# One of four subtractions as an adding DMA, in a graph-attention layer on one core

## The chip, the cores and the metric

The kernel runs on one core of a Trainium2 chip. A core has five engines that work side by side, each with its own queue of instructions in order: PE (TensorE, matrix products), DVE (VectorE), ACT (ScalarE), POOL (GpSimd) and SP (SyncE, which here issues DMAs). DMAs run on 16 DMA engines; SP's and POOL's DMAs are issued from those engines' queues. Engines wait for each other and for DMAs by semaphores. Data lies in SBUF (128 partitions), products in PSUM. The metric is the device time of one execution in microseconds (us); less is better.

## The reference

Four layers of a graph network over 32 graphs of 512 nodes with 64 features, all with the same adjacency matrix. The change touches only the last layer, a graph attention with eight heads and one output head:

```python
def gat_layer(x, graph, W, b):
    h = x @ W
    s = jnp.einsum('bnd,bmd->bnm', h, h) * graph
    s = jnp.where(s == 0.0, NEG_INF, s)
    a = jax.nn.softmax(s, axis=2)
    return jnp.einsum('bnm,bmd->bnd', a, h) + b
...
heads = jax.vmap(lambda W, b: gat_layer(flow_x, graph, W, b))(Wh, bh)
...
x = jax.nn.leaky_relu(cat, negative_slope=0.01)
out = gat_layer(x, graph, W_out, b_out)
return jax.nn.leaky_relu(out, negative_slope=0.01)
```

Each softmax needs, for each node, the greatest of its scores, which is subtracted before the exponential. Scores are symmetric, so the kernel takes maxima along one axis and subtracts them along the other.

## The kernel before

Layers 0 to 2 take the first 460 us or so. The rest is layer 3, as a pipeline of 144 units: 128 units of the class `Heads` (32 graphs, four units each, a unit being two heads of one graph) and 16 of `Out` (the output head of two graphs). A unit has scores of two 512x512 matrices, held as four row blocks r = 0 to 3; each block is a tile `p_att` of 128 partitions by 1024 floats (`self.p[r]`, from the pool `pbuf` of 14 buffers).

The steps of a unit:

- `scores(r)`: PE multiplies into the PSUM tile `s_ps` (two buffers).
- `maxima(r)` (L379): one DVE instruction for each half of the block writes the negated, masked scores to `p_att` and the least of each row, which is minus the greatest score, to a column of `top`.
- `spread_out` (L386, L389): DVE transposes `top` into `top_t`; SP writes it with four small DMAs to `top_row` in DRAM.
- `spread_in` (L395): SP loads that row, repeated on all 128 partitions, into `topb` (512 KB in SBUF, two buffers).
- `shift(r)` (L401): POOL subtracts `topb` from block r.
- `exps(r)` (L404): ACT takes exp(-p) of block r.
- `totals` (L420 to L432): PE sums the columns, DVE transposes the sums, ACT copies them to `parts`.
- `values(j)` (L410), `recips`, `normalize` (L438 to L450): PE multiplies with the values, DVE divides.
- `y_pe`, `y_act` (L538), `y_dve` (L546): PE multiplies with the head's weights, ACT and DVE make the leaky ReLU, `cat`.
- For the output: `product` (PE, L570), `keep_product`, `make_v`, `make_gs` (POOL, L589), `back`, `back_pool` (POOL), `store` (SP).
- `make_hx`, `make_g` (ACT copies, L522), `features` (small ACT steps) prepare later units.

The order is written out by hand. `flow_period(t)` emits the instructions of period t, and the order in which it emits them is the order on every engine's queue (the schedule is manual for all five engines). In period t, `now` is unit t, `unit(1)` the unit before, `unit(2)` the one before that, and `ahead` the next. So the maxima of blocks 2 and 3 of unit t and its `spread_out` and `spread_in` are emitted after `exps(0)`, `y_act` and `exps(1)` of `unit(1)`; then follow `y_dve`, the first maxima of the next unit, `shift(2)`, `exps(2)`, POOL's and SP's output steps, `totals`, `shift(3)`, `exps(3)`, and the rest. Waits between engines are put in by the framework from what is written and read.

`nc.gpsimd.dma_start` issues a DMA from POOL's queue; the kernel uses it before only for some weights at its start (L94 to L127).

Of the kernel before, what the change touches and what calls it, by code (L numbers as in the profile page):

```python
# [10 lines left out]
OP = mybir.AluOpType  # L11
# [3 lines left out]
P = 128  # L15
# [7 lines left out]
def fast_form(  # L23
# [25 lines left out]
    nc = tc.nc  # L49
    B, N, F = x.shape  # L50
    C = N // P
# [264 lines left out]
    class Pair:  # L316
# [67 lines left out]
        def spread_out(self):  # L384
            t = tiny.tile([P, 32], F32, name="top_t")
            nc.vector.transpose(t, self.top)  # L386
            self.top_row = dram.tile([2 * C, P], F32, name="top_row")
            for q in range(Q):
                nc.sync.dma_start(  # L389
                    self.top_row[:, q * 32 : (q + 1) * 32], t[q * 32 : q * 32 + 2 * C, :]  # L390
                )
# [6 lines left out]
            )  # L398

        def shift(self, r):  # L400
            nc.gpsimd.tensor_tensor(self.p[r], self.p[r], self.topb, OP.subtract)  # L401

        def exps(self, r):
            nc.scalar.activation(self.p[r], self.p[r], AF.Exp, scale=-1.0)  # L404
# [227 lines left out]
    def any_zero():  # L632

        def across(src, rows, name):
            ps = ps_m.tile([P, P], F32, name=name, tag="m")
            n = src.shape[0]
            nc.tensor.transpose(ps[:rows, :n], src, ident[:n, :n])
            return ps[:rows, :n]

        own = tiny.tile([P, 1], F32, name="own")  # L640
        nc.vector.tensor_reduce(own, least, AX.X, OP.min)
        two = tiny.tile([1, 2], F32, name="two")
        nc.vector.tensor_reduce(two[:, 0:1], across(own, 1, "own_ps"), AX.X, OP.min)
        best = tiny.tile([B // 2, 2], F32, name="best")
        nc.vector.tensor_reduce(
            best,
            across(least_out, B // 2, "out_ps").rearrange("b (k f) -> b k f", k=2),
            AX.X, OP.max,
        )
        worst = tiny.tile([B // 2, 1], F32, name="worst")  # L650
        nc.vector.tensor_reduce(worst, best, AX.X, OP.min)
        nc.vector.tensor_reduce(
            two[:, 1:2], across(worst, 1, "worst_ps"), AX.X, OP.min
        )
        flag = tiny.tile([1, 1], F32, name="flag")
        nc.vector.tensor_reduce(flag, two, AX.X, OP.min)
        nc.vector.scalar_tensor_tensor(
            again, flag, 0.0, unsound, op0=OP.is_equal, op1=OP.max
        )
# [6 lines left out]
    def planned(units, products):  # L666

        class Nothing:
            def __getattr__(self, name):
                return lambda *args: None  # L670

        nothing = Nothing()

        def period(t):
            def unit(lag):
                return units[t - lag] if 0 <= t - lag < len(units) else nothing

            now, ahead = unit(0), unit(-1)
            for r in range(2, C):
                now.scores(r)  # L680
            unit(3).y_pe()
            unit(1).shift(0)
            unit(1).exps(0)
            unit(3).y_act()
            if t - 1 in products:
                products[t - 1].keep_product()
            unit(1).shift(1)
            unit(1).exps(1)
            for r in range(2, C):
                now.maxima(r)  # L690
            now.spread_out()
            now.spread_in()
            for r in range(2):
                ahead.scores(r)
            unit(3).y_dve()
            for r in range(2):
                ahead.maxima(r)
            unit(-3).features(3)
            unit(3).back()
            unit(1).shift(2)  # L700
            unit(1).exps(2)
            unit(4).back_pool()
            unit(-2).make_gs()
            unit(4).store()
            unit(2).totals()
            unit(1).shift(3)
            unit(1).exps(3)
            for j in range(C):
                unit(2).values(j)
            u = products.get(t)  # L710
            if u:
                u.product()
            unit(2).recips()
            unit(3).back_dve()
            unit(2).normalize()
            unit(1).make_v()
            unit(-3).make_hx()
            unit(-2).make_g()
            for step in range(3):
                unit(step - 6).features(step)  # L720
            if t == len(units):
                any_zero()

        return period
# [1061 lines left out]
```

## Time and profile before

| What | Value |
|---|---|
| Median of 3 runs | 2175.14 us (2174.02 to 2175.47) |
| The profiled execution's own time | 2177.9 us |
| Its span, first to last instruction | 2176.1 us |
| Mean granted TensorE clock | 0.992 |
| `topb` loads | 144 of 512 KB |
| DMA queues' busy share (hardware queue q1) | 12.5% of 16 engines |
| POOL's subtraction, L401 | 576 times 2376 ns |
| ACT's exponential, L404 | 576 times 1057 ns |
| DVE's maxima, L379 | 1152 times 685 ns |

A row of the profile's groups gives line, engine, operation, the tile written and the tiles read, shapes and count, then busy time in us and the mean of one in ns, then the engine's idle time just before these instructions and what ended most of it. A row of a timeline gives the start in us from the span's start, how long the engine took for the merged group, engine, line, operation, tiles and count. "POOLq" and "SPq" are those engines' instruction sequencers, which issue DMAs. The chain of work that ended last is followed back from the last instruction, at each step to what released it.

### The profile page before, as it was taken

What the parts mean: (1) busy time and instruction counts of PE and PEld (TensorE: products, weight loads), DVE (VectorE), ACT (ScalarE), POOL (GpSimd) and SP (SyncE); (2) the same over time, 40 slices, a digit from 0 to 9 for tenths busy, and PEclk for the clock granted to TensorE, in tenths of its full rate; (3) what the DMA queues carried; (4) which work ended last, traced back from release to release, by engine and by line L of the source; (5) the groups of instructions that cost most, each with busy time, mean ns of one, the idle gap of its engine ahead of it and who ended that gap; (6) DMA issues with size and microseconds to landing.
All of it is one profiled execution on the core that took longest, in us unless ns stands there. A gap on an engine that the chain in (4) does not pass through costs nothing.

```text
span 2176.1 us, 34386 instructions
## 1 busy us (share of the span) xinstructions
PE 2108.7 (97%) x12190; PEld 840.5 (39%) x12190; DVE 1661.6 (76%) x4241; ACT 1294.9 (60%) x2520; POOL 1420.0 (65%) x665
## 2 busy tenths in 40 slices
PE   7999999989999999999999999999999999999996
PEld 4666776733333333333333333333333333333332
DVE  6799997668787877777777787877787787878774
ACT  3444433347676767675767676766676676766554
POOL 2000000048787878787878787878787877878786
PEclk9999999899999999999999999999999999999999
DMA  5000000001111111111111111111111111111112
GB/s 134 1 1 2 1 1 1 1 30 50 40 49 54 49 45 54 40 54 40 54 49 55 40 54 40 54 40 54 50 54 40 40 50 50 48 41 50 40 49 51
DMA packets 54565, 89.87 MB, mean 41 GB/s; under 512 B 30008, under 2 KB 35296, under 8 KB 54256
## 3 DMA queue, kind: packets, MB, share of 16 engines
q1 hardware_dynamic: 53872, 87.39, 12.5%
q8 instruction: 97, 1.59, 0.3%
q0 software_dynamic: 512, 0.20, 0.1%
q14 instruction: 84, 0.69, 0.1%
HBM read 81.73 MB, written 4.78 MB: 40 GB/s over the span
## 4 chain that ended last, share of the span: by engine, by line
PE 55%; DVE 27%; ACT 9%; POOL 3%; issue 3%; DMA 2%; DVEq 0%; SPq 0%; POOLq 0%; ACTq 0%
DVE p_att L379 15%; PE av L410 13%; PE nt_ps L833 7%; PE s_ps L367 7%; PE tot_ps L420 7%; PE acc L925 6%; PE gT_ps L570 5%; DVE cat L546 3%; POOL p_att L401 3%; PE g_ps L510 3%; ACT parts L432 2%; DVE recb L443 2%; DVE o_att L450 2%; ACT p_att L404 2%; DVE tot_t L427 2%
## 5 line engine op out<-in xcount | busy, mean ns | idle before, releaser
L401 POOL TENSOR_TENSOR p_att<-p_att,topb 128x1024 f32<-128x1024 f32 x576 | 1348.8, 2376 | 394.2 <-DMA topb<-top_row 254.4
L379 DVE CUSTOM_DVE_ANT_0 p_att<-s_ps,flow_neg 128x512 f32<-128x512 f32 x1152 | 724.5, 685 | 160.0 <-PE s_ps L367 159.9
L404 ACT ACTIVATE p_att<-p_att 128x1024 f32<-128x1024 f32 x576 | 607.1, 1057 | 216.5 <-POOL p_att L401 207.8
L367 PE MATMUL s_ps<-hx,g 64*128 64x512 f32 x2048 | 527.2, 612 | 17.5 <-ACT hn L474 5.8
L410 PE MATMUL av<-p_att,hn 128*64 128x512 f32 x2048 | 468.2, 599 | 0.0
L367 PEld LDWEIGHTS s_ps<-hx,g 64*128 64x128 f32 x2048 | 174.1, 185 | 322.3 <-DVE top L379 184.3
L420 PE MATMUL tot_ps<-p_att,ones 128*32 128x512 f32 x2304 | 281.2, 602 | 2.8 <-ACT p_att L404 2.5
L410 PEld LDWEIGHTS av<-p_att,hn 128*64 128x64 f32 x2048 | 135.8, 137 | 327.8 <-issue 327.8
L1001 POOL TENSOR_TENSOR x<-x,bias_b 128x512 f32<-128x512 f32 x16 | 20.3, 1275 | 280.1 <-DVE hn L775 280.1
L546 DVE SCALAR_TENSOR_TENSOR cat<-y_ps,bh,cat 128x512 f32<-128x512 f32 x256 | 177.8, 736 | 18.5 <-ACT cat L538 15.0
L538 ACT ACTIVATE cat<-y_ps,bh 128x512 f32<-128x512 f32 x256 | 160.8, 679 | 18.7 <-PE y_ps L528 17.9
L438 DVE TENSOR_REDUCE rec_flow<-parts 128x16 f32<-128x32 f32 x144 | 27.1, 188 | 176.1 <-ACT parts L432 176.1
L522 ACT COPY g<-g_ps 128x512 f32<-128x512 f32 x128 | 68.6, 588 | 154.0 <-PE g_ps L510 153.7
L430 ACT COPY parts<-tot_t 128x16 f32<-128x16 f32 x144 | 31.3, 217 | 181.4 <-DVE tot_t L427 181.4
L528 PE MATMUL y_ps<-o_att,wh_sb 64*128 64x512 f32 x512 | 133.5, 597 | 4.0 <-DVE o_att L450 3.1
L420 PEld LDWEIGHTS tot_ps<-p_att,ones 128*32 128x32 f32 x2304 | 60.5, 109 | 191.7 <-issue 108.2
L432 ACT COPY parts<-tot_t 32x16 f32<-32x16 f32 x576 | 123.8, 215 | 6.7
L925 PE MATMUL acc<-v,s 64*128 64x65 f32 x2048 | 124.2, 280 | 0.7 <-DVE s L911 0.4
L427 DVE STREAM_TRANSPOSE tot_t<-tot_ps 128x512 f32<-128x512 f32 x144 | 102.2, 710 | 29.1 <-PE tot_ps L420 29.1
L925 PEld LDWEIGHTS acc<-v,s 64*128 64x128 f32 x2048 | 121.3, 195 | 5.9 <-DVE o L941 1.2
L833 PE MATMUL nt_ps<-adj_t,hn 128*128 128x512 f32 x256 | 116.1, 596 | 0.8 <-DVE hn L797 0.8
L570 PE MATMUL gT_ps<-cat,wo_sb 128*64 128x512 f32 x512 | 112.6, 592 | 0.0
(176 smaller groups left out, 2021.8 us busy)
## 6 DMA issues: line engine op xcount, KB each, us to landing
topb<-top_row SPq DMA_DIRECT2D x144, 512.0 KB
top_row<-top_t SPq DMA_DIRECT2D x576, 1.0 KB
out_dram<-y SPq DMA_DIRECT2D x32, 128.0 KB
x<-in_x_dram SPq DMA_DIRECT2D x3, 1024.0 KB
x<-in_x_dram SPq DMA_DIRECT2D x4, 256.0 KB
adj_raw<-in_adj_dram SPq DMA_DIRECT2D x1, 1024.0 KB
mask<-mask SPq DMA_DIRECT2D x4, 256.0 KB
wh_sb<-in_L_gnn_Wh_dram SPq DMA_DIRECT2D x2, 256.0 KB
```

The costliest lines, as they stand in the source:

```text
L367: nc.tensor.matmul(ps[:, k], lhsT=g[halves(k), r * P : (r + 1) * P], rhs=x[halves(k), :], start=True, stop=True,)
L379: nc.vector.tensor_tensor_reduce(out=self.p[r][:, k], in0=ps[:, k], in1=flow_neg[:, r], scale=-1.0, scalar=BIG, op0=OP.add, op1=OP.min, ac ...
L401: nc.gpsimd.tensor_tensor(self.p[r], self.p[r], self.topb, OP.subtract)
L404: nc.scalar.activation(self.p[r], self.p[r], AF.Exp, scale=-1.0)
L410: nc.tensor.matmul(self.av[halves(k), :], lhsT=self.v(k, j), rhs=self.p[j][:, k], start=(j == 0), stop=(j == C - 1),)
L420: nc.tensor.matmul(ps[q : q + 32, :], lhsT=ones, rhs=self.p[j][:, k], start=(j < 2), stop=(j >= 2),)
L432: nc.scalar.copy(self.parts[q * 32 : (q + 1) * 32, 1], one[(q ^ 1) * 32 : ((q ^ 1) + 1) * 32])
L538: nc.scalar.activation(self.cat[:, k], self.y[k], AF.Identity, bias=bh01[:, h : h + 1], scale=0.01)
L546: nc.vector.scalar_tensor_tensor(self.cat[:, k], self.y[k], bh[:, h : h + 1], self.cat[:, k], op0=OP.add, op1=OP.max,)
L570: nc.tensor.matmul(ps[halves(k), :], lhsT=wo_sb[:, h, :], rhs=Heads.cat[self.b + k, h], start=(h == 0), stop=(h == H - 1),)
L833: nc.tensor.matmul(p, lhsT=lhs(k), rhs=adj_t[:, k, :], start=(k == 0), stop=(k == C - 1))
L925: nc.tensor.matmul(self.acc[k][:, r], lhsT=self.s[b // 2][halves(k), b % 2, r * P : (r + 1) * P], rhs=self.v[halves(k), b], start=(b == 0) ...
```

## The change

Three edits. The row of maxima is negated: after DVE's transpose, ACT multiplies `top_t` by -1, so that `top_row` and `topb` hold the negated row. POOL's subtraction of blocks 0, 1 and 2 becomes an addition. Block 3 is done by a DMA issued from POOL's queue, which reads the row from DRAM, repeated on 128 partitions, and adds it into `p_att`; it is emitted at the start of the period, ahead of `shift(0)`, instead of after `totals`. `exps(3)` stays where it was.

```diff
         def spread_out(self):
             t = tiny.tile([P, 32], F32, name="top_t")
             nc.vector.transpose(t, self.top)
+            nc.scalar.mul(t, t, -1.0)
             self.top_row = dram.tile([2 * C, P], F32, name="top_row")
...
         def shift(self, r):
-            nc.gpsimd.tensor_tensor(self.p[r], self.p[r], self.topb, OP.subtract)
+            if r < C - 1:
+                nc.gpsimd.tensor_tensor(self.p[r], self.p[r], self.topb, OP.add)
+            else:
+                nc.gpsimd.dma_start(
+                    self.p[r].rearrange("p k n -> p (k n)"),
+                    self.top_row.rearrange("(o r) p -> o (r p)", o=1).to_broadcast([P, 2 * N]),
+                    accum_op=OP.add,
+                )
...
             unit(3).y_pe()
+            unit(1).shift(3)
             unit(1).shift(0)
             unit(1).exps(0)
...
             unit(2).totals()
-            unit(1).shift(3)
             unit(1).exps(3)
```

## The prediction

> **What bounds the kernel now.** I read first the shares of the engines, then the chain of work that ended last, then the row of the instructions that the change touches. From the page:
>
> ```profile
> PE 2108.7 (97%) x12190; PEld 840.5 (39%) x12190; DVE 1661.6 (76%) x4241; ACT 1294.9 (60%) x2520; POOL 1420.0 (65%) x665
> ...
> PE 55%; DVE 27%; ACT 9%; POOL 3%; issue 3%; DMA 2%; DVEq 0%; SPq 0%; POOLq 0%; ACTq 0%
> ...
> L401 POOL TENSOR_TENSOR p_att<-p_att,topb 128x1024 f32<-128x1024 f32 x576 | 1348.8, 2376 | 394.2 <-DMA topb<-top_row 254.4
> ```
>
> PE is nearly always busy, and the chain runs mostly through PE and DVE. POOL, which is to be relieved, holds 3% of the chain, and its subtraction mostly waits for a DMA. So less POOL work is worth little; what counts is whether the change puts something new between the PE's periods.
>
> Next I asked for the rhythm, by the one transpose of the maxima that each of the 144 units has (view of its tile), and by SP's issues (timeline):
>
> ```profile
> L386 DVE STREAM_TRANSPOSE top_t<-top x144: 211/211/215, 460.9 to 2138.7; 128x32 f32<-128x32 f32 x144
> ```
>
> ```profile
> 1096.53 1.28 SPq L389 DMA_DIRECT2D top_row<-top_t  x4
> ...
> 1114.51 1.28 SPq L389 DMA_DIRECT2D top_row<-top_t  x4
> ...
> 1203.43 1.28 SPq L389 DMA_DIRECT2D top_row<-top_t  x4
> ```
>
> (2138.7 - 460.9) / 143 = 11.73 us a unit. One period in nine also holds the output product and takes 18.0 us (1096.53 to 1114.51); the eight after it take 88.9 here. Nine take 9 x 11.73 = 105.6, so an ordinary one takes (105.6 - 18.0) / 8 = 10.95. There are 144 / 9 = 16 such cycles.
>
> **Path of the maxima.** SP, POOL, ACT and DVE timelines around units that I call A and B:
>
> ```profile
> 1007.51 1.28 SPq L389 DMA_DIRECT2D top_row<-top_t  x4
> 1009.74 0.34 SPq L395 DMA_DIRECT2D topb<-top_row  x1
> 1018.43 1.28 SPq L389 DMA_DIRECT2D top_row<-top_t  x4
> 1020.75 0.34 SPq L395 DMA_DIRECT2D topb<-top_row  x1
> ```
>
> ```profile
> 1013.41 9.36 POOL L401 TENSOR_TENSOR p_att<-p_att,topb 128x1024 f32<-128x1024 f32 x4 [1.50 <-DMA topb<-top_row]
> 1024.40 9.37 POOL L401 TENSOR_TENSOR p_att<-p_att,topb 128x1024 f32<-128x1024 f32 x4 [1.62 <-DMA topb<-top_row]
> ```
>
> ```profile
> 1015.85 1.04 ACT L404 ACTIVATE p_att<-p_att 128x1024 f32<-128x1024 f32 x1
> ...
> 1018.15 1.06 ACT L404 ACTIVATE p_att<-p_att 128x1024 f32<-128x1024 f32 x1
> ...
> 1026.80 1.06 ACT L404 ACTIVATE p_att<-p_att 128x1024 f32<-128x1024 f32 x1 [0.84 <-POOL p_att L401]
> 1027.76 1.25 ACT L538 ACTIVATE cat<-y_ps,bh 128x512 f32<-128x512 f32 x2
> 1029.12 1.06 ACT L404 ACTIVATE p_att<-p_att 128x1024 f32<-128x1024 f32 x1
> ```
>
> ```profile
> 1018.19 0.21 DVE L386 STREAM_TRANSPOSE top_t<-top 128x32 f32<-128x32 f32 x1
> 1018.33 1.37 DVE L546 SCALAR_TENSOR_TENSOR cat<-y_ps,bh,cat 128x512 f32<-128x512 f32 x2
> ...
> 1028.45 0.21 DVE L386 STREAM_TRANSPOSE top_t<-top 128x32 f32<-128x32 f32 x1
> ```
>
> The reader is to see who waits for whom: B's top_row leaves 0.03 us after B's transpose (1018.40 to 1018.43), without regard to ACT. A's second exponential (1018.15) ends at 1019.21, 0.8 us **after** that transpose; B's ends at 1030.18, 1.5 us after the next one (1028.66).
>
> **The change part by part.**
>
> *The negation on ACT* costs 0.21 us (estimate between L471's ACTIVATE of 128x4 at 0.19 and L430's copy of 128x16 at 0.22). 144 x 0.21 = 30 us of ACT work are not the point; its place is. ACT runs in order, and the program emits exps(0), y_act, exps(1) of the unit before ahead of spread_out. So the negation of B waits for A's second exponential, and SP's four top_row writes, then topb, then POOL's first add and the adding DMA wait for the negation. Behind it on ACT stand exps(2), the totals' copies, exps(3), the copies of g; behind the waiting top_row writes on SP only topb and now and then two stores of y, which nothing waits for before the end. This closes a loop that wasn't there: second exponential of A, negation of B, top_row, topb, two POOL adds, second exponential of B. Once round:
>
> - first top_row issue to topb issue: 2.23 (1007.51 to 1009.74);
> - topb issue to the first add: 3.67 and 3.65 here, 3.96 at 1098.76 to 1102.72; I take 3.80;
> - first add to second exponential: 4.74 (1013.41 to 1018.15); the exponential 1.06;
> - negation 0.21, two hand-overs 0.05 + 0.03.
>
> Sum 12.12 us, against an ordinary period of 10.95. The loop, not PE, sets the ordinary period.
>
> *The adding DMA.* On POOL it replaces an add of 2.38 us with an issue; the nearest rows are 0.76 and 0.52:
>
> ```profile
> 1.29 0.76 POOL L105 DMA_DIRECT2D bias_b<-in_L_gnn_bias_dram  x1 [0.35 <-issue]
> ```
>
> ```profile
> bias_b<-in_L_gnn_bias_dram POOLq DMA_DIRECT2D x1, 32.0 KB, 7.3
> ...
> bh_raw<-in_L_gnn_bh_dram POOLq DMA_DIRECT2D x1, 4.0 KB, 5.4
> ```
>
> It stands ahead of the three adds, gs and the back adds, but starts when top_row has landed, as topb does, so its 0.8 us hide in topb's 3.80; without that cover they would be 0.8 us of every loop. POOL loses 144 x (2.38 - 0.76) = 233 us of work that nothing waited for: worth 0, at most a quarter of POOL's 3% (16 us).
>
> It moves a second 512 KB beside topb. Topb's own transfer fills some 2.2 us (the DMA share is nonzero from 1021.7 to 1023.9). Bounds for topb's delay: 0, if the new packets come after it (software DMAs took 5.4 us and more from issue to landing, topb 3.7), and 1.8, if both share evenly from 0.4 us after topb's start (0.76 against 0.34 us of issuing). The landing rows are nearer to 0; I take 0.4. The loop is then 12.5.
>
> The Trainium skill, "DMA: Bandwidth & Descriptors", section "Issuing engines are not separate DMA queues", speaks against the change here: DMAs of all issuers share the same 16 engines and interleave. By its fabric ceiling, 512 KB would delay topb by 1.2 us (an estimate from that page); at 1.2 the loop would be 13.3 and the sum 2425.
>
> Its landing is needed by exps(3), the fourth exponential. Landing plus ACT's work from there to the next negation but one (fourth exponential 1.06, g 1.07, hn 1.06, first exponential 1.06, cat 1.25, second exponential 1.06, negation and hand-overs 0.3, top_row 2.23: 9.1) has two periods, 25.0: it decides only from 15.9 us after top_row's landing. 5.4 to 8.7 (rows of software DMAs) plus one or two times 2.2 is 7.6 to 13.1: hidden.
>
> **From loop to span.** The lateness can't be kept from PE: DVE's cat waits for y_act, which stands on ACT behind exps(0). First add to the end of cat is 5.4 (1024.40 to 1027.76, + 1.25 + 0.71); from cat's end (1019.70) to the end of the next transpose (1028.66) 8.96. So a transpose comes no earlier than 14.3 us after the first add one unit before. The second exponential ends 5.8 after that add, so it runs at most 12.5 + 5.8 - 14.3 = 4.0 us behind the transpose. After the long period it is 1.6 behind, since ACT was held by g until 1111.9:
>
> ```profile
> 1115.03 2.03 ACT L404 ACTIVATE p_att<-p_att 128x1024 f32<-128x1024 f32 x2
> ```
>
> (the first of the two ends at 1116.1, the transpose at 1114.5). The long period thus gives back 4.0 - 1.6 = 2.4. A cycle: 8 x 12.5 + 18.0 - 2.4 = 115.6, or 10.0 more than 105.6. Times 16: +160. The profiled execution took 2177.9 (span 2176.1 and 1.8 around it), so 2338; it lies 2.8 above the median of 2175.14, so **2335**.
>
> **Rivals.**
>
> 1. *PE runs freely ahead* (the coupling by cat is looser). Then the loop alone bounds the mean: (12.12 - 11.73) x 144 = 56, or 2231; with the delay of 0.4, 2289. For it: 14 p buffers, three and a half units. Against it: DVE's queue is in order.
> 2. *The adding DMA lands late*: nothing in the trace adds by DMA. At 20 us the period would be (20 + 9.1) / 2 = 14.6; (14.6 - 12.5) x 8 x 16 = 269 on top: about 2600. It decides from 15.9.
> 3. *Not slower*: the negation finds ACT free, since the second exponential ends before the transpose, and POOL's relief shortens the chain. Worth up to 16 us: 2159, or nothing: 2175. It needs topb's landing at least 1.5 us earlier than now; for it only that POOL is sometimes the late one, against it that the first add mostly waits for DMA.
> 4. *The overlap is full* (delay 1.8): loop 13.9, a cycle 111.2 + 18.0 - 3.8 = 125.4, 19.8 x 16 = 317: 2492.
>
> **How the numbers follow.** The loop sets the period, with a delay of 0 to 1.3: 67%, 2335, own range 2290 (12.1: 96.8 + 16.0 = 112.8, +115) to 2436. Free PE 12%; late landing 7%; full overlap 5%; not slower 9%. The range 2235 to 2480 leaves out rivals 2, 3 and 4, 2 in 10. Faster by over 0.2% (what a measurement here can tell; the runs spread by 0.07%) 5%, within 0.2% 4%, slower 91%.
>
> **What would show it.** ACT's negation is released in most periods by ACT itself (it directly follows the second exponential), not by DVE; from transpose to top_row there are 2 to 4 us instead of 0.03; ordinary periods are 12 to 13 us, long ones near 16 to 18; PE's share falls to about 90%; topb issue to first add shows the delay. Wrong if the transposes keep 10.95 apart, if the fourth exponential waits for the DMA, or if POOL's issue takes over 3.8 us.

## The result and the profile after

The changed kernel takes 2363.72 us (median of 4 runs, 2358.5 to 2364.43), beside 2175.3 for the kernel before. The ratio is 1.086, 95% interval 1.084 to 1.088: slower by 188 us. The profiled execution has a span of 2362.6 us.

From the page, the lines that answer to those of before:

```profile
PE 2167.6 (92%) x12190; PEld 836.5 (35%) x12190; DVE 1663.5 (70%) x4241; ACT 1315.4 (56%) x2664; POOL 1210.3 (51%) x665
...
PE 29%; DMA 25%; POOL 22%; DVE 7%; issue 6%; ACT 5%; SPq 4%; ACTq 0%; POOLq 0%; DVEq 0%
...
L403 POOL TENSOR_TENSOR p_att<-p_att,topb 128x1024 f32<-128x1024 f32 x432 | 1010.3, 2360 | 422.1 <-DMA topb<-top_row 418.8
...
L405 POOL DMA_DIRECT2D p_att<-top_row x144 | 127.4, 885 | 404.0 <-ACT hs L494 148.7
...
p_att<-top_row POOLq DMA_DIRECT2D x144, 512.0 KB, 7.4
```

POOL did get lighter, from 1420 to 1210 us, and nothing came of it. The chain has turned round: POOL and DMA, 5% of it before, now hold 47%, and PE and DVE have fallen from 82% to 36%. The engine that was relieved is now on the chain, because what stands on it waits for something new. PE's busy time rose by 59 us for the same 12190 instructions, and its mean granted clock fell from 0.992 to 0.981. No run sets the clock apart, but neg_only below is 126 us slower than the kernel before with its clock at 0.986 to 0.990, and ties_off has 0.982 and is 49 us faster than the changed kernel.

The rhythm, by the transposes and the negations (view of the tile `top_t`; min/median/max in ns, then first and last start):

```profile
L386 DVE STREAM_TRANSPOSE top_t<-top x144: 211/211/214, 463.5 to 2319.6; 128x32 f32<-128x32 f32 x144
L387 ACT ACTIVATE top_t<-top_t x144: 208/213/239, 463.7 to 2322.6; 128x32 f32<-128x32 f32 x144
```

(2319.6 - 463.5) / 143 = 12.98 us a unit, against 11.73. Of the 186.5 us that the span grew, 178 lie between the first and the last transpose, 3 ahead of them and 6 behind.

The loop itself stands in the chain of waits of the changed kernel (start, duration, what; us, the shorter pieces left out):

```profile
1101.91 0.22 ACT top_t L387
...
1104.37 4.09 DMA topb<-top_row
...
1108.54 4.71 POOL p_att L403 x2
...
1114.23 0.22 ACT top_t L387
...
1116.70 4.19 DMA topb<-top_row
...
1120.97 4.70 POOL p_att L403 x2
```

The same steps come round again after 12.32 us, and from 1090 to 1135 no PE and no DVE stand among them. Why the negation comes so late is seen on DVE and ACT (timelines):

```profile
1110.42 0.21 DVE L386 STREAM_TRANSPOSE top_t<-top 128x32 f32<-128x32 f32 x1
```

```profile
1113.27 1.06 ACT L412 ACTIVATE p_att<-p_att 128x1024 f32<-128x1024 f32 x1
1114.23 0.21 ACT L387 ACTIVATE top_t<-top_t 128x32 f32<-128x32 f32 x1
```

The transposed maxima are there at 1110.63. ACT takes them up at 1114.23, 3.6 us later, directly behind the second exponential of the unit before. So it is in 142 of the 143 units that follow another. The instruction costs 0.21 us; its place in the queue costs 3.6.

### The profile page after: what moved, and what is told of

Same layout as the page of the kernel before. It is cut to its first block, busy times and chain, and to the rows that moved or that the text cites. A ratio compares the mean times of both kernels' runs of the same rounds, so it can differ in the third digit from the quotient of the medians.

```text
span 2362.6 us, 34786 instructions
## 1 busy us (share of the span) xinstructions
PE 2167.6 (92%) x12190; PEld 836.5 (35%) x12190; DVE 1663.5 (70%) x4241; ACT 1315.4 (56%) x2664; POOL 1210.3 (51%) x665
## 3 DMA queue, kind: packets, MB, share of 16 engines
q0 software_dynamic: 21248, 75.71, 18.5%
q1 hardware_dynamic: 53872, 87.39, 12.8%
## 4 chain that ended last, share of the span: by engine, by line
PE 29%; DMA 25%; POOL 22%; DVE 7%; issue 6%; ACT 5%; SPq 4%; ACTq 0%; POOLq 0%; DVEq 0%
POOL p_att L403 22%; DMA topb<-top_row 20%; PE nt_ps L841 7%; DMA top_row<-top_t 5%; PE acc L933 5%; PE gT_ps L578 5%; SPq L390 4%; DVE p_att L379 3%; PE av L418 3%; PE s_ps L367 2%; PE tot_ps L428 2%; ACT p_att L412 2%; PE po L860 1%; ACT cat L546 1%; DVE cat L554 1%
## 5 line engine op out<-in xcount | busy, mean ns | idle before, releaser
L403 POOL TENSOR_TENSOR p_att<-p_att,topb 128x1024 f32<-128x1024 f32 x432 | 1010.3, 2360 | 422.1 <-DMA topb<-top_row 418.8
L367 PE MATMUL s_ps<-hx,g 64*128 64x512 f32 x2048 | 541.3, 627 | 38.5 <-DVE top L379 20.9
L405 POOL DMA_DIRECT2D p_att<-top_row x144 | 127.4, 885 | 404.0 <-ACT hs L494 148.7
L428 PE MATMUL tot_ps<-p_att,ones 128*32 128x512 f32 x2304 | 287.0, 613 | 2.1 <-ACT p_att L412 1.9
L536 PE MATMUL y_ps<-o_att,wh_sb 64*128 64x512 f32 x512 | 142.5, 633 | 95.4 <-DVE o_att L458 94.5
```

The costliest lines, as they stand in the source:

```text
L367: nc.tensor.matmul(ps[:, k], lhsT=g[halves(k), r * P : (r + 1) * P], rhs=x[halves(k), :], start=True, stop=True,)
L428: nc.tensor.matmul(ps[q : q + 32, :], lhsT=ones, rhs=self.p[j][:, k], start=(j < 2), stop=(j >= 2),)
L536: nc.tensor.matmul(ps, lhsT=wh_sb[halves(k), 2 * self.i + k, :], rhs=self.o[halves(k), :], start=True, stop=True,)
```

## The experiments

The first three take the loop apart; the others try ways round it and follow what did not come out.

**Negation on ACT alone, without the adding DMA (neg_only).**

```diff
             nc.vector.transpose(t, self.top)
+            nc.scalar.mul(t, t, -1.0)
...
-            nc.gpsimd.tensor_tensor(self.p[r], self.p[r], self.topb, OP.subtract)
+            nc.gpsimd.tensor_tensor(self.p[r], self.p[r], self.topb, OP.add)
```

> The kernel before with only the negation on ACT and POOL adding instead of subtracting; no adding DMA, all four blocks on POOL at their old places. Theory: the loop alone, with topb undisturbed (3.8 us from issue to first add): ordinary period 12.1 us, 2290 us. Rival (the DMA is the cost): 2175 to 2200 us. The rest, from here to the changed kernel's 2364, is the price of the DMA.

2302.39 us, 1.059 times the kernel before (1.056 to 1.062), 12 us above what was expected. From topb's issue to the first add there are 3.80 us (median; 3.84 in the kernel before). The loop alone makes 126 of the 188 us; the other 62 come with the adding DMA, with which that wait is 4.30 us.

**Three negations (neg_thrice).**

```diff
             nc.scalar.mul(t, t, -1.0)
+            nc.scalar.mul(t, t, -1.0)
+            nc.scalar.mul(t, t, -1.0)
```

> The changed kernel with the negation done three times on ACT (same result), 0.42 to 0.52 us more in the loop and 30 us of ACT work twice more. Theory: each us in the loop costs 7 us in a cycle of nine, 112 us in all, so +47 to +58 us: 2411 to 2422 us, ordinary periods about 13.1 us. Rival (ACT's negation is covered, something else sets the period): within 10 us of 2364.

2422.82 us (ratio 1.114, 1.112 to 1.116), 59 more than the changed kernel, at the upper end of what was expected. From the start of the first negation to the end of the last there are now 0.74 us (median) where there were 0.21, since there are short gaps between the three: 0.52 us more in the loop. So time put into the loop is paid at 59 / 0.52 = 113 us for each us, as expected: seven periods in each of 16 cycles, 112 in all. ACT's work itself is not the price: ACT has 44% of its time free, and in neg_only 31 us of it cost 126 us.

**The second exponential behind the negation (exps1_late).**

```diff
             unit(1).shift(1)
-            unit(1).exps(1)
...
             now.spread_out()
+            unit(1).exps(1)
```

> The changed kernel with the second exponential emitted after the negation instead of ahead of it. Theory: the loop then goes through the first exponential and y_act, 11.55 instead of 12.64 us, and the time is 2225 us (2190 to 2260), with the adding DMA unchanged. Rival (the adding DMA sets the time): no less than 2340 us.

2237.37 us (1.027, 1.025 to 1.029). ACT's timeline shows the negation ahead of the exponential:

```profile
1106.76 0.23 ACT L387 ACTIVATE top_t<-top_t 128x32 f32<-128x32 f32 x1
1106.97 1.06 ACT L412 ACTIVATE p_att<-p_att 128x1024 f32<-128x1024 f32 x1
```

One line moved in the order of the queue takes back 126 of 188 us, with every DMA, add and negation still there. The 61 us that are left fit the shorter loop that was expected, 12 us above the middle of its range.

**Negation on DVE (neg_dve).**

```diff
-            nc.scalar.mul(t, t, -1.0)
+            nc.vector.tensor_scalar(t, t, -1.0, None, op0=OP.mult)
```

> The changed kernel with the negation on DVE, right after its transpose, instead of ACT. Theory (the loop through ACT's queue sets the period): the loop is gone, ordinary periods fall from 12.6 back to about 10.95 us, top_row's issue follows the transpose by about 0.3 us, and the time is 2175 to 2200 us (DVE has one small instruction more, 0 to 0.2 us in 144 periods), although the adding DMA is still there. Rival (the adding DMA itself is the cost, by contention or late landing): it stays above 2290 us.

2247.67 us (1.033, 1.031 to 1.035): neither. The loop is gone, yet 71 us remain. The view of `top_t` shows where:

```profile
L387 DVE TENSOR_SCALAR top_t<-top_t x144: 181/812/2364, 462.8 to 2202.7; 128x32 f32<-128x32 f32 x144
```

An instruction that takes 181 ns at best takes 812 at the median, and at most 2364, as long as one POOL add. DVE's and POOL's timelines show one case:

```profile
1010.56 1.25 DVE L387 TENSOR_SCALAR top_t<-top_t 128x32 f32<-128x32 f32 x1
```

```profile
1007.10 7.02 POOL L403 TENSOR_TENSOR p_att<-p_att,topb 128x1024 f32<-128x1024 f32 x3 [2.78 <-DMA topb<-top_row]
```

The second of POOL's three adds starts at 1009.42 and ends at 1011.77; DVE's negation, begun at 1010.56, ends at 1011.81. It is the rule: 114 of the 144 negations take over 0.3 us, each of them began while a POOL add ran, and each ends 0.04 to 0.05 us after the end of one.

**The same without the adding DMA (neg_dve_only).**

```diff
             nc.vector.transpose(t, self.top)
+            nc.vector.tensor_scalar(t, t, -1.0, None, op0=OP.mult)
...
-            nc.gpsimd.tensor_tensor(self.p[r], self.p[r], self.topb, OP.subtract)
+            nc.gpsimd.tensor_tensor(self.p[r], self.p[r], self.topb, OP.add)
```

> The kernel before with only the negation on DVE, POOL adding all four blocks, no adding DMA. In the run with DVE's negation and the adding DMA that instruction took 181 to 2364 ns, and ended with POOL's running add. Theory (DVE's negation can't run beside a POOL add and waits for its end): 2215 to 2260 us, the instruction again at a median of 0.5 us or more. Rival (the 72 us that remained there were the adding DMA's): 2176 to 2190 us.

2261.83 us (1.039, 1.037 to 1.041): 85 us without any adding DMA, with four POOL adds to run into instead of three. The instruction's median is 461 ns, its greatest 4770, two adds long. So the 71 us of the run before need no adding DMA; how much of them is this wait is seen in the next pair of runs.

**Negation by a DVE reduction (neg_reduce, neg_reduce_only).**

```diff
-            nc.scalar.mul(t, t, -1.0)
+            turned = t
+            t = tiny.tile([P, 32], F32, name="top_neg")
+            nc.vector.tensor_reduce(t, turned[:, :, None], AX.X, OP.min, negate=True)
```

The second kernel has the same lines in the kernel before, with `OP.add` in all four shifts.

> The changed kernel with the negation as a DVE reduction over one element with its negate flag (same result), instead of ACT. A DVE reduction of this size took 0.19 us in the profile, and unlike the scalar multiplication on DVE it is not expected to wait for POOL's running add. Theory: the instruction takes 0.2 us throughout, no loop; what is left is that POOL's first add comes some 0.7 us later (0.2 the reduction, 0.5 the adding DMA beside topb's): 2190 to 2215 us. Rival (any DVE instruction there waits for POOL): 2240 to 2260 us, as with the scalar multiplication.

> The kernel before with only this negation by a DVE reduction, POOL adding all four blocks, no adding DMA. Theory: 2176 to 2195 us, so that the difference to the run with the adding DMA is the adding DMA's own price without any loop, 10 to 30 us. Rival (the DVE instruction is what costs): within 5 us of the run with the adding DMA.

2195.64 us with the adding DMA (1.0088, 1.0073 to 1.0102) and 2185.53 without (1.0048, 1.0034 to 1.0062). The view of the tile in the first:

```profile
L389 DVE TENSOR_REDUCE top_neg<-top_t x144: 185/186/190, 461.1 to 2154.0; 128x32 f32<-128x32 f32 x144
```

The same 128x32 elements, negated on the same engine at the same place, never wait, though 126 of the 144 began while a POOL add ran. (The reduction also writes a tile of its own; the scalar form was not run that way.) Without a loop and without that wait, the negation costs 10 us and the adding DMA another 10. Against neg_dve, 71 - 20 = 51 us were the wait. The Trainium skill has a rule that fits both forms ("SBUF — State Buffer", section "Who interferes with whom"): DVE and GpSimd share one pair of SBUF ports as an exclusive lock, which a scalar operation on DVE may take and a reduction never takes. The waits above agree with it; that the ports are the cause is the page's word, and no run here shows it.

**The adding DMA behind the second add (dma_third).**

```diff
-            unit(1).shift(3)
             unit(1).shift(0)
             unit(1).exps(0)
...
             unit(1).shift(1)
+            unit(1).shift(3)
             unit(1).exps(1)
```

> The changed kernel with the adding DMA emitted after shift(1) on POOL instead of ahead of shift(0), so that its packets follow topb's. Theory: topb issue to first add falls from 4.30 to about 3.8 us, the loop from 12.6 to 12.1, and the time to 2290 to 2330 us; the DMA lands some 13 us after the first add's start at the latest, which may make the fourth exponential wait. If topb's delay does not matter: 2364 us. If the late landing decides: slower than 2364 us, with the fourth exponential waiting for the DMA.

2531.09 us (1.162, 1.160 to 1.165): a miss, and for neither of the reasons named. Topb's wait did fall to 3.80 us, and the adding DMA landed sooner, 5.0 us after its issue instead of 7.4. The fourth exponential waited for that landing in 7 units only, 4.0 us in all. SP's timeline shows the new cost, POOL's the adding DMA that it meets:

```profile
1143.07 1.58 SPq L390 DMA_DIRECT2D top_row<-top_t  x4
1147.82 0.34 SPq L396 DMA_DIRECT2D topb<-top_row  x1
1157.41 1.48 SPq L390 DMA_DIRECT2D top_row<-top_t  x4
1161.92 0.34 SPq L396 DMA_DIRECT2D topb<-top_row  x1
```

```profile
1141.77 0.90 POOL L405 DMA_DIRECT2D p_att<-top_row  x1
...
1156.11 0.87 POOL L405 DMA_DIRECT2D p_att<-top_row  x1
```

The writes of the next top_row, 1 KB each, are issued from 1143.07, while the adding DMA issued at 1141.77 is under way until about 1146.8. They need 4.75 us until topb can be issued (4.4 at the median of all units), where the median is 2.2 to 2.3 in the other kernels. The chains of waits have the step itself, here and in the changed kernel:

```profile
1144.32 3.37 DMA top_row<-top_t
```

```profile
1103.13 1.16 DMA top_row<-top_t
```

The trace also records each DMA's packets, the pieces in which it moves. In the changed kernel the first small packet of a top_row moves 0.74 us after SP's first issue; here it moves 2.98 us after it (medians), when the adding DMA's last 4 KB packets run. So the writes stood behind the adding DMA. The loop grew by more than the other place had cost it: the mean period is 14.13 us.

**A row of its own for the adding DMA (own_row), and that with the second exponential late (own_row_early).**

```diff
-            nc.scalar.mul(t, t, -1.0)
+            self.t = t
...
         def spread_in(self):
...
+            neg = tiny.tile([P, 32], F32, name="top_neg")
+            nc.scalar.mul(neg, self.t, -1.0)
+            self.neg_row = dram.tile([2 * C, P], F32, name="neg_row")
+            for q in range(Q):
+                nc.sync.dma_start(
+                    self.neg_row[:, q * 32 : (q + 1) * 32], neg[q * 32 : q * 32 + 2 * C, :]
+                )
```

POOL subtracts again in blocks 0 to 2, and the adding DMA reads `neg_row`. The second kernel also has `exps(1)` behind `spread_in`.

> The changed kernel with a row of its own for the adding DMA: topb's row stays as before (POOL subtracts blocks 0 to 2), ACT's negation writes a second small tile, which SP writes to a second row in DRAM after it has issued topb. So the negation still stands behind the second exponential on ACT, but only the adding DMA waits for it. Theory (the cost was the loop, to a third topb's delay by the adding DMA): topb issue to first add is back at 3.8 us, since the adding DMA starts some 2 us later, the period is 10.95, and the time 2165 to 2190 us. Rival (the adding DMA costs by itself, through POOL's queue or the fourth exponential): 2230 us or more.

> The run with a row of its own for the adding DMA, and the second exponential emitted after the negation, so that the negated row lands some 1.5 us earlier. In the earlier run topb issue to first add was 4.98 us, because POOL's first add stands behind the adding DMA's issue, which waited for the negated row (4.37 us after topb's issue, plus 0.88), and its packets still ran when the next top_row was written. Theory (these two waits were all that was left): the adding DMA is issued some 2.6 us after topb, the first add is back at 3.8 to 4.0, the ordinary period at 10.95, and the time is 2170 to 2190 us. Rival (the adding DMA costs elsewhere too): 2210 us or more.

2227.46 us (1.025, 1.023 to 1.027) and 2219.45 us (1.021, 1.020 to 1.022): both misses, the second within its rival's range. Top_row leaves 0.03 us after its transpose again, so the loop is gone, yet topb's issue to the first add takes 4.98 and 4.92 us instead of 3.8. An earlier negation did not help, as SP and POOL show in the second kernel:

```profile
1081.99 0.34 SPq L396 DMA_DIRECT2D topb<-top_row  x1
1082.46 1.28 SPq L404 DMA_DIRECT2D neg_row<-top_neg  x4
```

```profile
1086.40 0.88 POOL L412 DMA_DIRECT2D p_att<-neg_row  x1 [2.28 <-ACT parts L447]
```

The small writes of `neg_row` are issued at once behind topb, but POOL gets its DMA off only at 1086.40, when topb has landed too, and the first add stands behind that issue. The packets show why: SP issues these writes from 0.5 us after topb on, but their last small packets move together with topb's last 4 KB packet, 3.3 us after topb's issue, and POOL's issue follows 1.0 us later (medians of the second kernel). So 45 to 51 us remain without a loop. The first add is 1.1 to 1.2 us late, and the second exponential starts 5.01 us after it, where the changed kernel has 4.72; no run separates what each costs.

**The ties between POOL's first add and DVE (cat_first, ties_off).** A tie here is a DVE instruction that waits for an ACT instruction which itself stands behind an exponential, and so behind POOL's adds.

```diff
-            unit(1).exps(0)
             unit(3).y_act()
+            unit(1).exps(0)
```

The second kernel has this and:

```diff
+            unit(2).totals()
             unit(1).shift(2)
             unit(1).exps(2)
...
-            unit(2).totals()
```

> The changed kernel with y_act emitted ahead of the first exponential, so that DVE's cat no longer waits behind it. Theory (the long period gives back little, since cat ties DVE and PE to POOL's first add): without the tie the mean period falls from 12.98 towards the loop's 12.64, so about 2315 us (2295 to 2335). If the tie is another one: 2354 to 2374 us, as the changed kernel.

> The changed kernel with y_act ahead of the first exponential, as in the run before, and the totals (with ACT's copies to parts) ahead of the third subtraction and exponential. In the run with y_act alone moved, DVE's reciprocals waited 116 us in 500 for these copies, which stand behind the third exponential on ACT. Theory (that was the second tie between POOL's first add and DVE): the mean period falls from 12.95 to about the loop's 12.64, 2295 to 2325 us. If a third tie holds: 2340 us or more.

2355.7 us (1.082, 1.081 to 1.084) and 2314.81 us (1.064, 1.063 to 1.066). Moving `y_act` away alone gained 8 us instead of 49, as the rival of another tie had it. ACT's and DVE's timelines of that kernel show what holds DVE next:

```profile
1109.20 1.06 ACT L412 ACTIVATE p_att<-p_att 128x1024 f32<-128x1024 f32 x1 [1.16 <-POOL p_att L403]
1110.17 0.20 ACT L438 COPY parts<-tot_t 128x16 f32<-128x16 f32 x1
```

```profile
1111.30 0.19 DVE L446 TENSOR_REDUCE rec_flow<-parts 128x16 f32<-128x32 f32 x1 [3.31 <-ACT parts L440]
```

The copies of the totals stand on ACT behind the third exponential, which waits for POOL's third add; DVE idles 3.31 us for them. With the totals moved as well, the mean period is 12.66, the loop's own length, and the time is where it was expected for the loop alone.

## Why the prediction was right

Forecast 2335 us (2235 to 2480), measured 2363.72. By its steps:

- *What bounds the kernel, and POOL's relief worth nothing*: right. 233 us less of POOL's work were forecast, 210 came; the span shows no gain, and neg_reduce, without the loop, is no faster than neg_reduce_only either. Of the 254.4 us that POOL's subtraction waited for topb before, 151.4 are one wait ahead of the first unit; the reading holds even so, since 120 of the 144 first subtractions start within 4.1 us of topb's issue.
- *The loop through the negation's place on ACT*: right, and shown from three sides. More in it costs (neg_thrice), a shorter way round it gives back (exps1_late), and with the reduction and no loop the same DMA and POOL work is within 1% of the kernel before (neg_reduce).
- *The terms of the loop*: top_row to topb 2.23 forecast, 2.24 measured (median); topb to first add with the adding DMA 4.2, measured 4.30; first add to second exponential 4.74, measured 4.72; negation 0.21, measured 0.213. The second exponential and its hand-over were put at 1.11; from its start to the negation's there are 0.96. That error and the 0.1 on topb's wait nearly cancel: the ordinary loop of 12.5, taken from one second exponential to the next without the long periods, was 12.47 at the median and 12.60 at the mean.
- *The adding DMA*: the delay of topb, taken as 0.4 between 0 and 1.8, is 0.50 (4.30 against 3.80 in neg_only). At 113 us for each us that is some 56 of the 62 us that the adding DMA adds. Its issue, 0.89 us, is hidden in topb's wait, and its landing, 7.4 us after the issue, comes at least 4.7 us before the fourth exponential; no wait of ACT on it shows in the changed kernel. The rule of the Trainium skill that was weighed there ("DMA: Bandwidth & Descriptors", section "Issuing engines are not separate DMA queues") is right that the two meet (the adding DMA lands after 7.4 us beside topb and after 5.0 in dma_third), but the estimate of 1.2 from that page's fabric ceiling was too high; the measurement decides for 0.5.
- *From loop to span*: the size was right, the reason half. The second exponential was to end at most 4.0 us behind the transpose and 1.6 after a long period; it ends 3.8 and 1.6 behind (medians). (The 5.4 in that working adds up to 5.3; the 14.3 drawn from it is right.) But cat, named as the tie, is only one of two nearly equal ones: without it the totals' copies hold DVE just as long (cat_first), and only without both does the loop stand alone (ties_off).
- *The sum*: 160 us forecast, 188 measured. The units make up 178. The forecast took all 16 cycles alike, at nine units and 10 us each. The first three took 44 us more than before instead of 30: the first long period is 24.3 us instead of 18.6, the next two 19.3 and 19.2 instead of 18.0. The other thirteen took 134 instead of 130. Another 6 us lie after the last transpose, where the forecast had put nothing, and 3 ahead of the first, in layers that the change doesn't touch; there the first transpose starts anywhere from 458.7 us (cat_first) to 464.7 (dma_third).

Of the rivals, free running of PE came true only once both ties were cut; the late landing, the full overlap and "not slower" did not come.

## What to carry to other kernels

An instruction costs its place in an in-order queue before it costs its time: look up what stands ahead of it there, and whether what it releases leads back to that same thing one period later. If so, a loop is closed, and its length, added up from the rows of the profile, is the period to expect where it exceeds the old one. Work taken off an engine that nothing waits for is worth nothing, and a transfer taken as free should be placed on the clock among the small transfers that others wait for, not only beside the large one.

## What the runs showed of the hardware

- A scalar multiplication of 128x32 floats on DVE waited for POOL's running add: 181 ns at best, 812 at the median, 2364 at most, and 4770 with four adds per unit; the 114 that took over 300 ns each ended 40 to 50 ns after a POOL add. A reduction of the same elements took 185 to 190 ns throughout, 126 times with a POOL add running.
- An adding DMA of 512 KB from POOL's queue landed 5.0 us after its issue when topb was not under way (dma_third), and 7.4 us when it was (the changed kernel); its issue held POOL for 0.88 us. In the changed kernel topb's first packet moves 0.98 us after its issue, the adding DMA's 2.28 us after its own. There, the transfers of all 144 (75.7 MB) took 18.5% of the DMA engines' time, those of the hardware queue (87.4 MB, topb mostly) 12.8%.
- Writes of 1 KB that met such a transfer took 4.4 us at the median instead of 2.2 until the DMA that depends on them could be issued; their first packet moved 2.98 us after the issue instead of 0.74. Writes of 1 KB issued just behind a plain 512 KB load on the same queue had their last packets moved with the load's last, 3.3 us after its issue.
